# First layer of a four-layer image network: taps in pairs, transposes on VectorE, TensorE in a written order

## The chip, the cores and the metric

The kernel runs on one core of a Trainium2 chip. The metric is the device time of one execution in microseconds; the time of a version is the median of its runs.

## What is computed

Two images of 512 channels and 64 x 64 pixels pass through four attention and pooling layers in float32, each added to its input after a group normalisation. Only the first layer is touched. Its reference, cut to what matters:

```python
q_norm = l2norm(q)                                   # per pixel and head: 8 heads of 64 channels
q_scaled = (q_norm + query_embedding) * softplus(temperature)
k_local = l2norm(k)                                  # then padded, and taken at 3 x 3 neighbours
attn_local = einsum('bhnd,bhndk->bhnk', q_scaled, k_local_patches)     # 9 taps
attn_pool = einsum('bhnd,bhpd->bhnp', q_scaled, l2norm(k_pool))        # 256 pooled keys
attn = softmax(concat([attn_local, attn_pool]))
a_local, a_pool = attn[..., :9], attn[..., 9:]
lt = einsum('bhnd,hdk->bhnk', q_norm, learnable_tokens) + learnable_bias + a_local
x_local = einsum('bhnk,bhndk->bhnd', lt, v_local_patches)
x_pool = einsum('bhnp,bhpd->bhnd', a_pool, v_pool)
out = (x_local + x_pool) @ W_proj + b_proj
```

## The kernel before

An image lies in the on-chip memory as four chunks of 128 channels (two heads each) by 4096 pixels. The class `Local` does the first layer. It cuts a chunk into four units of 1024 pixels (16 image rows), so an image has 16 units. A unit is worked in halves of 512 pixels, the width of one accumulator bank.

`run` is a software pipeline. In each turn of its loop the work of several units is laid side by side as Python generators, and `in_turn` takes one step of each, round after round. In turn `i`, `projections` makes the keys of unit `i+4`, the queries of unit `i+3` and the values of unit `i+1`; `norms` and `normed` normalise what the turn before projected; `tap_products` and `tap_sums` make the nine neighbour scores of unit `i+1`; `attend` does the pooled attention and the softmax denominators of unit `i`; `weigh` applies the nine neighbour weights of unit `i-1`. The loop runs from -4 to 16; turns 0 to 15 have an `attend`.

The order in which the generators emit their instructions is a priority. A scheduler then lays out a fixed sequence for each engine: it takes an instruction when it holds it to be ready, earlier emitted ones first. So on TensorE the work of the stages is interleaved as the scheduler saw fit, not as it is written. Every engine runs its own sequence strictly as laid out and waits on semaphores. All transfers in this part are issued by SyncE's queue.

The steps that the change touches:

- Norms (L2275 to L2308). A product with a 0/1 matrix puts the sums of squares of up to four half units into rows 0 and 1 of four strips of 32 partitions of one bank. ScalarE copies the bank (L2279), TensorE transposes it in four 128 x 128 blocks (L2283), VectorE computes the inverse root in integer and float steps on 32 columns (L2290 to L2298) into the array `wide`, TensorE transposes `wide` back (L2304) and ScalarE copies it (L2306). `normed` spreads two rows over the 128 channels by a product (L2318) and multiplies on VectorE (L2326). `learned` (L2339) makes the token scores and the scaled queries.
- Taps (L2366, L2379). VectorE multiplies the unit's queries with the keys shifted by one tap, 1024 columns at a time, into a ring of three buffers `prods`; TensorE sums each over the channels of a head, two taps at a time into four strips of one bank.
- Denominators (L2433, L2437, L2458). The exponentials of two key blocks are added on GpSimd (L2426), for the second half in place in the exponentials' own buffer; TensorE sums them over keys, into rows that alternate between the two heads, so that 64 rows per half hold only two different values each; VectorE inverts all 512 columns, in two halves.
- Weighing (L2491 to L2510). Each tap's weight is spread to the partitions by a transfer (L2477) into a ring of three buffers, copied to an accumulator bank by ScalarE, multiplied on VectorE and added on GpSimd (L2504).

Accumulator memory: five banks `mm` are shared by the projections, scores, `values`, norms, spreads and the weighing's copies; one bank holds the tap sums, two hold the queries for the tap products.

Of the kernel before, what the change touches and what calls it, by code (L numbers as in the profile page):

```python
# [1914 lines left out]
class Local:  # L1915
# [9 lines left out]
    def __init__(self, net, X, Y, sp_scale, d, wp, yp, pp, ppt, pps):  # L1925
# [20 lines left out]
        self.prods = [whole.take([P, self.UT])] + [new([P, self.UT], f"prod{i}") for i in range(2)]  # L1946
# [19 lines left out]
        self.qn = new([P, self.UT], "qn")  # L1966
# [3 lines left out]
        self.wide = new([P, NT, P], "wide")  # L1970
# [12 lines left out]
        nc.gpsimd.memset(self.wide, 0.0)  # L1983
# [11 lines left out]
    def run(self):  # L1995
# [10 lines left out]
        for i in range(-4, units + 1):  # L2006
# [22 lines left out]
            in_turn(*stages)  # L2029
# [139 lines left out]
    def fetch_output(self):  # L2169

        for _ in range(3):

            yield
        for kc in range(KC):
            self.nc.sync.dma_start(self.sq[kc], self.d["W_proj"][kc * P:(kc + 1) * P, :])
        self.pb = self.kp[:, :2, :].rearrange("p c n -> p (c n)")
        self.nc.sync.dma_start(self.pb, self.d["pb_rows"])
        yield

    def output(self, c4):  # L2180
# [4 lines left out]
        toks = ([self.prods[0], self.prods[1], self.prods[2], self.qs[(units - 2) % 3]] if c4 % 2  # L2185
# [46 lines left out]
    def projections(self, uk, uq, uvs, streams):  # L2232
# [33 lines left out]
    def norms(self, streams, ended):  # L2266
# [27 lines left out]
        for i in range(3):  # L2294
            nc.vector.tensor_tensor(a, n, y, ALU.mult)
            nc.vector.tensor_tensor(a, a, y, ALU.mult)
            dst = self.wide.rearrange("p t (s r) -> p t s r", s=4)[:, :, :, :2] if i == 2 else y
            nc.vector.scalar_tensor_tensor(dst, a, 1.5, y, ALU.add, ALU.mult)  # L2298
        yield
        yield  # L2300
        yield
        ps = self.bank()
        for t in range(NT):
            nc.tensor.transpose(ps[:, t * P:(t + 1) * P], self.wide[:, t, :], self.net.ident)  # L2304
        rows = wp.tile([P, TB], F32, name="n_rows")
        nc.scalar.copy(rows, ps)  # L2306
# [3 lines left out]
    def normed(self, ended):  # L2310

        nc = self.nc
        for _ in range(5):
            yield
        for which in "kq":
# [11 lines left out]
            yield  # L2327
        if mine:
# [27 lines left out]
    def tap_products(self, u):  # L2356
# [5 lines left out]
        qs = qs.rearrange("p (y x) -> p y x", x=W)  # L2362
        y = u % self.UN * self.UY
        for k in range(9):
            dy, dx = divmod(k, 3)
            self.nc.vector.tensor_tensor(  # L2366
                self.prods[k % 3].rearrange("p (y x) -> p y x", x=W), qs,
                self.kx[:, y + dy:y + dy + self.UY, dx:dx + W], ALU.mult)
            yield

    def tap_sums(self, u):
# [3 lines left out]

        def sums(k):
            for j in range(2):
                q = 2 * j + k % 2
                nc.tensor.matmul(ps[32 * q:32 * q + 32, :],  # L2379
                                 self.cst[:, C_TAPW + 16 - 2 * k:C_TAPW + 48 - 2 * k],  # L2380
                                 self.prods[k % 3][:, j * TB:(j + 1) * TB], start=(k < 2),
                                 stop=(k > 6))

        yield
        yield
        for k in range(0, 8, 2):
            sums(k)
            sums(k + 1)
            yield
            if k < 6:  # L2390
                yield
        sums(8)
# [5 lines left out]
    def attend(self, u):  # L2398
# [45 lines left out]
        yield  # L2444
        values(0)
        yield
# [254 lines left out]
```

## Time and profile before

| | |
|---|---|
| median of 5 runs | 5157.76 us (5148.33 to 5165.67) |
| the profiled execution | 5172.35 us, its span 5170.4 us |
| TensorE / VectorE / ScalarE / GpSimd busy | 95 / 59 / 36 / 36% of the span |
| mean granted TensorE clock | 0.978 of full speed |
| first layer's loop, denominators of unit 0 to those of unit 13 | 575.54 us (first image) |

The profile is of one execution. The duration of a TensorE product in it is modelled, and products overlap: the price of a group is the distance from its first start to the start of the next group. A product in float32 appears as two instructions. The tile names `late`, `big` and `mm` are the shared work area, the two image arrays (whose free one lends space to this layer) and the five banks. "Idle before" is the time that an engine waited, with the instruction that released it.

### The profile page before, as it was taken

What the parts mean: (1) busy time and instruction counts of PE and PEld (TensorE: products, weight loads), DVE (VectorE), ACT (ScalarE), POOL (GpSimd) and SP (SyncE); (2) the same over time, 40 slices, a digit from 0 to 9 for tenths busy, and PEclk for the clock granted to TensorE, in tenths of its full rate; (3) what the DMA queues carried; (4) which work ended last, traced back from release to release, by engine and by line L of the source; (5) the groups of instructions that cost most, each with busy time, mean ns of one, the idle gap of its engine ahead of it and who ended that gap; (6) DMA issues with size and microseconds to landing.
All of it is one profiled execution on the core that took longest, in us unless ns stands there. A gap on an engine that the chain in (4) does not pass through costs nothing. (4 is left out here: it accounts for less than half of the span.)

```text
span 5170.4 us, 48736 instructions
## 1 busy us (share of the span) xinstructions
PE 4907.3 (95%) x17299; PEld 2039.7 (39%) x17299; DVE 3068.0 (59%) x3986; ACT 1864.7 (36%) x3547; POOL 1846.5 (36%) x1216
## 2 busy tenths in 40 slices
PE   7999999899998999999999999998999999999998
PEld 3423332555333444433344333335543344444333
DVE  4266777644579633478732677776445795334766
ACT  1245665324422233322112556652343232333221
POOL 0035566500430045454500455565003200454544
PEclk9999999899999999999999999999999999999999
DMA  3035556600000000211120355565000000000111
GB/s 149 2 81 133 145 141 170 171 27 10 1 1 17 1 1 1 66 49 46 60 73 2 93 138 144 144 169 163 19 10 1 1 17 1 1 1 21 39 45 44
DMA packets 124752, 309.88 MB, mean 60 GB/s; under 512 B 20882, under 2 KB 33682, under 8 KB 122964
## 3 DMA queue, kind: packets, MB, share of 16 engines
q1 hardware_dynamic: 124500, 306.68, 21.0%
q8 instruction: 139, 2.28, 0.2%
q14 instruction: 113, 0.93, 0.1%
HBM read 258.11 MB, written 48.50 MB: 59 GB/s over the span
## 5 line engine op out<-in xcount | busy, mean ns | idle before, releaser
L134 PE MATMUL mm<-big,w 128*128 128x512 f32 x2496 | 1164.0, 611 | 9.1 <-DVE late L2458 9.1
L134 PEld LDWEIGHTS mm<-big,w 128*128 128x128 f32 x2496 | 456.4, 192 | 678.2 <-issue 561.5
L2504 POOL TENSOR_TENSOR late<-late,big 128x1024 f32<-128x1024 f32 x192 | 454.4, 2367 | 192.2 <-DVE big L2499 175.3
L1616 POOL TENSOR_TENSOR big<-big 128x512 f32<-128x512 f32 x224 | 278.0, 1274 | 219.2 <-ACT big L1607 219.2
L2426 POOL TENSOR_TENSOR late<-late 128x512 f32<-128x512 f32 x128 | 160.7, 1278 | 516.0 <-ACT late L2415 494.4
L2499 DVE TENSOR_TENSOR big<-big,mm 128x512 f32<-128x512 f32 x384 | 255.8, 682 | 126.9 <-ACT mm L2491 112.9
L2491 ACT COPY mm<-big 128x512 f32<-128x512 f32 x428 | 244.5, 593 | 179.6 <-DMA big<-rows 144.9
L1607 ACT ACTIVATE big<-mm,ed 128x256 f32<-128x256 f32 x512 | 194.0, 490 | 232.7 <-DVE top L1603 200.3
L2504 POOL TENSOR_TENSOR late<-late,tap 128x1024 f32<-128x1024 f32 x96 | 227.3, 2368 | 103.9 <-DVE tap L2499 99.0
L1420 POOL TENSOR_TENSOR wq<-prob 128x512 f32<-128x512 f32 x48 | 70.9, 1501 | 511.3 <-ACT prob L1417 511.3
L1871 PE MATMUL mm<-k,w 128*128 128x512 f32 x512 | 236.8, 606 | 12.4 <-DVE k L1864 7.4
L1603 DVE TENSOR_REDUCE top<-mm 128x1 f32<-128x512 f32 x256 | 159.1, 684 | 148.3 <-PE mm L1535 148.3
L134 PE MATMUL mm<-big,wq 128*128 128x512 f32 x512 | 236.8, 612 | 2.7 <-ACT off_t L1219 2.7
L2366 DVE TENSOR_TENSOR prod<-qs,big 128x1024 f32<-128x1024 f32 x192 | 230.7, 1217 | 8.8 <-PE tap L2379 6.8
L1191 PE MATMUL mm<-big,wo 128*128 128x512 f32 x512 | 234.7, 604 | 0.0
L1581 PE MATMUL mm<-w,big 128*128 128x512 f32 x512 | 234.5, 601 | 0.0
L1346 PE MATMUL acc<-big,diag 128*128 128x512 f32 x512 | 226.6, 601 | 4.6 <-ACT diag L1344 4.6
L1861 DVE RECIPROCAL psD<-psD 128x512 f32<-128x512 f32 x64 | 215.1, 3362 | 1.9
L969 POOL TENSOR_TENSOR group_stats<-group_stats,cst 128x1 f32<-128x1 f32 (+1 forms) x20 | 12.2, 624 | 570.9 <-DVE group_stats L968 539.4
L2379 PE MATMUL tap<-prod,cst 128*32 128x512 f32 x768 | 199.1, 605 | 8.9 <-DVE prod L2366 8.0
L134 PE MATMUL mm<-big,big 128*128 128x512 f32 x464 | 201.7, 594 | 0.5 <-DVE b_sr L1007 0.5
L1417 ACT ACTIVATE prob<-mm 128x512 f32<-128x512 f32 x256 | 133.0, 602 | 171.6 <-PE mm L1414 171.3
(410 smaller groups left out, 8488.5 us busy)
## 6 DMA issues: line engine op xcount, KB each, us to landing
big<-rows SPq DMA_DIRECT2D x428, 256.0 KB, 4.3
tap<-rows SPq DMA_DIRECT2D x212, 256.0 KB, 4.2
yd<-late SPq DMA_DIRECT2D x32, 512.0 KB, 2.9
lost_all<-lost SPq DMA_DIRECT2D x128, 128.0 KB, 3.1
out<-big SPq DMA_DIRECT2D x64, 256.0 KB, 2.0
big<-in_W_kv SPq DMA_DIRECT2D x8, 1024.0 KB, 8.8
rows<-late SPq DMA_DIRECT2D x64, 128.0 KB, 2.3
big<-yd SPq DMA_DIRECT2D x16, 512.0 KB, 5.1
```

What stands on the lines that cost most here:

```text
L134: self.nc.tensor.matmul(ps, w[:, kc, :], X[:, kc, blk * TB:(blk + 1) * TB], start=(kc == 0), stop=(kc == KC - 1))
L1191: nc.tensor.matmul(ps, w[:, kc, oc * P:(oc + 1) * P], att[:, kc, :], start=(kc == 0), stop=(kc == KC - 1))
L1346: nc.tensor.matmul(accs[b], dg, src[:, b * TB:(b + 1) * TB], start=(j == 0), stop=(j == 6))
L1581: nc.tensor.matmul(ps, X[:, kc, lo:lo + P], wv[:, kc, :], start=(kc == 0), stop=(kc == KC - 1))
L1616: nc.gpsimd.tensor_tensor(a, a, part, ALU.add)
L1861: nc.vector.reciprocal(psD, psD)
L1871: nc.tensor.matmul(ps, self.wo[:, kc, oc * P:(oc + 1) * P], qs[:, kc, :], start=(kc == 0), stop=(kc == KC - 1))
L2366: self.nc.vector.tensor_tensor(self.prods[k % 3].rearrange("p (y x) -> p y x", x=W), qs, self.kx[:, y + dy:y + dy + self.UY, dx:dx + W], A ...
L2379: nc.tensor.matmul(ps[32 * q:32 * q + 32, :], self.cst[:, C_TAPW + 16 - 2 * k:C_TAPW + 48 - 2 * k], self.prods[k % 3][:, j * TB:(j + 1) * ...
L2491: nc.scalar.copy(ps, part)
L2499: nc.vector.tensor_tensor(part.rearrange("p (y x) -> p y x", x=W), self.vx[:, y:y + self.UY // 2, dx:dx + W], ps.rearrange("p (y x) -> p y ...
L2504: nc.gpsimd.tensor_tensor(out, out, t, ALU.add)
```

## The change

Four things are changed in `Local`.

The tap products are made two taps at a time: one VectorE instruction over 2 x 1024 columns, with the queries repeated and the keys read at two shifts (`shifted`), into a ring of two buffers of two taps (`pair`). The ninth tap stays alone.

The norms lose both sets of TensorE transposes, both ScalarE copies and the array `wide`. VectorE transposes the bank in place in 32 x 32 blocks, computes the roots in the first columns of each block, and transposes the bank into the buffer `sq[3]`.

The denominators are transposed in place on VectorE in 32 x 32 blocks, so that in each block of 32 columns two hold all the different values; these 32 columns in all are inverted, and a second transpose that reads each pair 16 times writes the full array `recip`.

In turns 0 to 13 TensorE's instructions are laid out in the order in which they are written, and the steps at which the stages emit them change. The fetch of the projection weights in turn 13 starts four steps later, and `qn` and the taps' buffers change places in memory.

```diff
-        self.prods = [whole.take([P, self.UT])] + [new([P, self.UT], f"prod{i}") for i in range(2)]
+        self.prods = [new([P, 2, self.UT], f"prods{i}") for i in range(2)]
...
-        self.qn = new([P, self.UT], "qn")
+        self.qn = whole.take([P, self.UT])
...
-            in_turn(*stages)
+            if 0 <= i < units - 2:
+                with self.net.tc.manual_schedule(engines={mybir.EngineType.PE}):
+                    in_turn(*stages)
+            else:
+                in_turn(*stages)
...
-        for _ in range(3):
+        for _ in range(7):
...
         for step in range(10):
-            if step >= 6:
-                project((uk, uq)[step // 2 - 3], "kq"[step // 2 - 3], step % 2)
-            if step % 3 == 0 and values:
+            if step in (4, 6, 7, 8):
+                i = (4, 6, 7, 8).index(step)
+                project((uk, uq)[i // 2], "kq"[i // 2], i % 2)
+            if step in (0, 2, 5, 9) and values:
...
-        rows = wp.tile([P, TB], F32, name="n_rows")
-        nc.scalar.copy(rows, ps)
-        yield
-        ps = self.bank()
-        for t in range(NT):
-            nc.tensor.transpose(ps[:, t * P:(t + 1) * P], rows[:, t * P:(t + 1) * P],
-                                self.net.ident)
-        sums = ps.rearrange("p (t s r) -> p t s r", t=NT, s=4)
-        n, a = (sums[:, :, :, 2 * i:2 * i + 2] for i in range(2))
-        y = wp.tile([P, NT, 4, 2], F32, name="roots")
+        yield
+        nc.vector.transpose(ps, ps)
+        n, a = (ps.rearrange("p (b r) -> p b r", r=32)[:, :, 2 * i:2 * i + 2] for i in range(2))
+        y = wp.tile([P, TB // 32, 2], F32, name="roots")
...
-            dst = self.wide.rearrange("p t (s r) -> p t s r", s=4)[:, :, :, :2] if i == 2 else y
-            nc.vector.scalar_tensor_tensor(dst, a, 1.5, y, ALU.add, ALU.mult)
-        yield
-        yield
-        yield
-        ps = self.bank()
-        for t in range(NT):
-            nc.tensor.transpose(ps[:, t * P:(t + 1) * P], self.wide[:, t, :], self.net.ident)
-        rows = wp.tile([P, TB], F32, name="n_rows")
-        nc.scalar.copy(rows, ps)
+            nc.vector.scalar_tensor_tensor(n if i == 2 else y, a, 1.5, y, ALU.add, ALU.mult)
+        rows = self.sq[3]
+        nc.vector.transpose(rows, ps)
...
-        for _ in range(5):
+        for _ in range(3):
             yield
...
             yield
+        yield
         if mine:
             self.learned(mine[-1][0][3])
...
-        for k in range(9):
-            dy, dx = divmod(k, 3)
+        for k in range(0, 9, 2):
+            n = min(2, 9 - k)
             self.nc.vector.tensor_tensor(
-                self.prods[k % 3].rearrange("p (y x) -> p y x", x=W), qs,
-                self.kx[:, y + dy:y + dy + self.UY, dx:dx + W], ALU.mult)
-            yield
+                self.pair(u, k)[:, :n].rearrange("p k (y x) -> p k y x", x=W),
+                bcast(qs.rearrange("p (y x) -> p y x", x=W), 1, n),
+                self.shifted(u % self.UN * self.UY, k, n), ALU.mult)
+            yield
+            if n == 2:
+                yield
+
+    def pair(self, u, k):
+        return self.prods[(5 * u + k // 2) % 2]
+
+    def shifted(self, y, k, n):
+        a = self.kx[:, y:y + self.UY, :W]
+        at = lambda k: k // 3 * (W + 2) + k % 3
+        part, rows, cols = a.ap
+        return bass.AP(a.tensor, a.offset + at(k), [part, [at(k + 1) - at(k), n], rows, cols])
...
+        yield
+        for k in range(0, 9, 2):
+            for i in range(min(2, 9 - k)):
+                for j in range(2):
+                    q = 2 * j + i
+                    nc.tensor.matmul(ps[32 * q:32 * q + 32, :],
+                                     self.cst[:, C_TAPW + 16 - 2 * (k + i):][:, :32],
+                                     self.pair(u, k)[:, i, j * TB:(j + 1) * TB],
+                                     start=(k == 0), stop=(k + i > 6))
+            for _ in range((2, 2, 3, 1, 0)[k // 2]):
                 yield
...
         exponentials(0, 1)
         yield
+        yield
         values(0)
-        yield
         exponentials(1, 0)
         yield
         exponentials(1, 1)
         yield
         values(1)
         yield
-        yield
         psD = sums()
-        for i in range(2):
-            part = slice(i * TB // 2, (i + 1) * TB // 2)
-            nc.vector.reciprocal(self.recip[:, part], psD[:, part])
+        nc.vector.transpose(psD, psD)
+        two = psD.rearrange("p (b n r) -> p b n r", n=16, r=2)[:, :, 0]
+        nc.vector.reciprocal(two, two)
+        nc.vector.transpose(self.recip.rearrange("p (b n r) -> p b n r", n=16, r=2),
+                            bcast(two, 2, 16))
         yield
         el = self.el.pop(u)
         nc.vector.tensor_tensor(el, el, self.recip, ALU.mult)
         nc.vector.tensor_tensor(el, el, self.lt.pop(u), ALU.add)
+        yield
         self.spread = self.rows()
```

More of the change, by code (lines that the diff above doesn't have):

```diff
@@ L1969, in __init__ @@
         self.half = new([P, 32], "mhalf32")
-        self.wide = new([P, NT, P], "wide")
         self.qb = new([P, KC], "qe_scaled")
@@ L1982, in __init__ @@
         nc.vector.memset(self.half, -0.5)
-        nc.gpsimd.memset(self.wide, 0.0)
         nc.vector.tensor_tensor(self.qb, self.vec[:, V_QE:V_QE + KC], sp_scale, ALU.mult)
@@ L2184, in output @@
         units = KC * self.UN
-        toks = ([self.prods[0], self.prods[1], self.prods[2], self.qs[(units - 2) % 3]] if c4 % 2
+        toks = ([a[:, i] for a in self.prods for i in range(2)] if c4 % 2
                 else [self.kraw, self.qn,
```

14 lines of the change are left out of this document (removed).

## The prediction

> **What bounds the kernel now.** I read the page's first block, then the busy time in chosen stretches, then TensorE's timeline inside one stretch, and last GpSimd's timeline there.
>
> ```profile
> span 5170.4 us, 48736 instructions
> ...
> PE 4907.3 (95%) x17299; PEld 2039.7 (39%) x17299; DVE 3068.0 (59%) x3986; ACT 1864.7 (36%) x3547; POOL 1846.5 (36%) x1216
> ```
>
> 95% is an average. The change touches only the first layer's loop over 16 units, twice (two images). The denominators' first product (L2433) starts at 306.50 us in the first unit and at 882.04 in the fourteenth; for the second image at 2880.44 and 3452.09. So 13 turns of the loop take 575.54 and 571.65 us: 44.27 and 43.97, mean 44.12 us a turn.
>
> ```profile
> 306.50:882.04 575.54, 563.72 (x2043) 184.51 (x2041) 412.45 (x642) 340.56 (x598) 330.13 (x165) 0.99 0.55 143
> ```
>
> The columns are length, then busy time of TensorE, its weight loads, VectorE, ScalarE, GpSimd. TensorE is busy 98%, VectorE 72%, GpSimd 57%. What ends a turn is TensorE's list of work, so the timeline must say whether that list can shrink and whether it is packed.
>
> ```profile
> 655.31 0.63 PE L2379 MATMUL tap<-prod,cst 128*32 128x512 f32 x3
> 655.75 0.59 PE L2379 MATMUL tap<-big,cst 128*32 128x512 f32 x1
> 655.76 0.61 PE L2379 MATMUL tap<-prod,cst 128*32 128x512 f32 x3
> 656.30 0.66 PE L2304 MATMUL mm<-cst,wide 128*128 128x128 f32 x4
> 656.88 1.94 PE L2421 MATMUL mm<-late,vp 128*64 128x512 f32 x8
> 658.90 1.13 PE L2318 MATMUL mm<-n_rows,cst 2*128 2x512 f32 x4
> 659.96 3.70 PE L134 MATMUL mm<-big,w 128*128 128x512 f32 x8
> 663.59 1.13 PE L2318 MATMUL mm<-n_rows,cst 2*128 2x512 f32 x4
> 664.65 1.94 PE L2433 MATMUL mm<-late,cst 128*64 128x512 f32 x8
> ...
> 671.15 1.07 PE L2339 MATMUL mm<-qn,big 128*32 128x512 f32 x8
> 672.05 1.02 PE L2379 MATMUL tap<-prod,cst 128*32 128x512 f32 x2
> ```
>
> Read the starts, not the durations: a group's price is the next start minus its own. Four transposes cost 0.58 us, `values` 1.9, a projection 3.64, two norm spreads 1.06, a denominators' first part 1.87 (the second, L2437, 1.00), the tokens' product (L2339) 0.90. Two taps together cost 0.99 and a lone tap 0.95: four strips of 32 columns run side by side and a lone tap fills two of them. Elsewhere in this turn scores of one half and key block (L2411) cost 1.06, sums of squares (L2276) 1.00.
>
> **The change part by part.** I count one turn of TensorE in the new order: six projections 21.84, four score groups 4.24, four tap pairs and one lone tap 4.91, `values` twice 3.74, norm spreads twice 2.12, denominators 2.87, tokens 0.90, sums of squares 1.00. Sum 41.62 us. Against 44.12 that is 2.50 us a turn, in three pieces.
>
> *Transposes go.* L2283 and L2304, two groups of four at 0.58: 1.16 us a turn, all on the path. Two ScalarE copies of 0.59 go too; ScalarE is 59% busy, worth nothing by itself.
>
> *Taps stay paired.* The present order issues about three pairs and three lone taps a turn, 5.82 us against 4.91: 0.91 us, if the written order holds.
>
> *The rest, 0.43 us*, is today's idle and slow-clock time, which goes only if the new order has none.
>
> *VectorE's list.* Removed: two reciprocals at 1.726 (3.45 us). Added: a transpose, a 32-column reciprocal, a transpose, and two transposes for the norms. No row has a bare transpose; the nearest is the transposing sum.
>
> ```profile
> L1799 DVE TRANSPOSE_TENSOR_REDUCE sq_cols<-sq 128x16 f32<-128x512 f32 x64 | 43.9, 694 | 26.6 <-POOL sq L1504 25.9 <-PE mm L1810 0.7
> L2458 DVE RECIPROCAL late<-mm 128x256 f32<-128x256 f32 x64 | 107.8, 1726 | 11.5 <-PE mm L2437 11.0
> ```
>
> [...] The reciprocal of 512 columns (L1861) is 3.362, of 256 is 1.726: 6.39 ns a column and 0.09 fixed, so 0.30 for 32. New: 4 x 0.69 + 0.30 = 3.06, against 3.45. Taps: nine at 1.217 become four of about 2.28 (1.066 us per 1024 elements, 0.15 fixed) and one of 1.217, so 10.34 for 10.95. [...] The denominators' own chain, sums to `el`, shortens from 3.45 to 1.7 us.
>
> On the pairing: VectorE is 72% busy here, and in the layout below no pair falls due sooner than some 10 us after its buffer is free. [...] I go by the row and charge nothing.
>
> *Steps moved.* The denominators and `el` come one step earlier, while the spread's two transfers and the first two fetches stay in steps eight and nine: SyncE's queue keeps its order against the weighing's fetches, but `el` waits up to a step in it; rows land about as early in the turn as now, so nothing. Norm spreads and tokens come one to two steps earlier, so their four multiplications (0.68) and the 1.24 us rescaling on ScalarE move forward into time when those engines are no busier. Projections are parted by spreads and denominators, so their ScalarE copies (0.69 and 0.68) bunch less. I charge these nothing; without that cover one step of each would cost a bank wait, which (c) below bounds.
>
> *The fixed order.* 14 turns of each image. Laid out by the prices above, from the first scores at 0: scores, value 4.7; squares 5.7, scores 6.8, taps 7.8; value 11.4; `values` 13.3, scores 14.3, taps 15.3, key spread 16.4; scores 17.4, projection 21.1, query spread 22.1; `values` 24.0, taps 25.0; denominators 27.9, projection 31.5, tokens 32.4; projection 36.0; taps, projection 40.7; last tap 41.6. What TensorE may now wait for, and everything behind it on TensorE waits too:
>
> (a) Denominators after `values`. They need GpSimd's sum of the two key blocks in place, so it starts only after `values` at 24.0. Only a tap pair, 1.0 us, lies between. Today `values` end at about 658.8 and the denominators start at 664.65, and in between GpSimd does this:
>
> ```profile
> 658.29 2.37 POOL L2504 TENSOR_TENSOR late<-late,tap 128x1024 f32<-128x1024 f32 x1 [2.72 <-DVE tap L2499]
> 660.62 2.51 POOL L2426 TENSOR_TENSOR late<-late 128x512 f32<-128x512 f32 x2
> ```
>
> GpSimd idle: the second head's sum lands 2.5 us after `values`, wait about 0.4. A tap addition of 2.37 just begun: 2.8. I take 0.8 (57% busy, half an addition left).
>
> (b) Key spread. Today the norms run from the transposes' end at 602.5 to the last root at 610.94: 8.4 us, mostly other VectorE work let in between. With a transpose on each side 9.8 us, against 9.6 between squares' end and key spread. Bounds 0 and 2; I take 0.3.
>
> (c) Five banks for scores, spreads and weighing copies around 13 to 18 us. Bounds 0 and 1.5; I take 0.3.
>
> Period 41.62 + 1.4 = 43.0 us, 1.1 less than now: 28 turns, 31 us.
>
> *Outside the fixed turns.* Three more turns an image lose 1.16 of transposes and about 1 us of waits around the two copies (0.76, 0.82, 0.99 and 0.73 us of idle are seen at 232 to 268): six turns, 12 us less 3 for transposes in sequence. The last turns lose idle behind the long reciprocal (2.68 us at 886, 2.92 at 3456), partly paid back: 3 us. The projection weights fetched four steps later have some 15 us before use: nothing. Together 12.
>
> **Sum.** The profiled execution took 5172.35 us, span 5170.4, the five runs' median 5157.76: the profile is 0.3% long. 31 + 12 = 43 us: 5129 in a profile, 5115 in the median.
>
> **The rivals.**
>
> *No waits at all.* If GpSimd is always free at 24 us and VectorE's norms keep time, the turn is 41.62: 2.50 x 28 + 15 = 85 us, 5073. For: today's waits on TensorE in ten turns sum to a few us. Against: (a) is too tight for zero.
>
> *Weighing becomes the bound.* Fetches for a unit begin at 636.17 and its output transfer issues at 679.45: 43.3 us, three buffers, each reused only after its GpSimd addition; the next unit's fetch went out after that. The long reciprocal held one step back some 2 us, which goes. If the chain keeps 43.3, later turns follow it or the lag lands in the last turns: 0.8 x 28 less some lag, about 10 to 20 us gained, 5143.
>
> *Slower.* The place is (a). TensorE did stop once for long in the early turns:
>
> ```profile
> 384.62 0.63 PE L2304 MATMUL mm<-cst,wide 128*128 128x128 f32 x4 [2.09 <-DVE wide L2298]
> 385.18 2.92 PE L2421 MATMUL mm<-late,vp 128*64 128x512 f32 x8
> 388.03 2.08 PE L2318 MATMUL mm<-n_rows,cst 2*128 2x512 f32 x4
> 390.04 6.77 PE L134 MATMUL mm<-big,w 128*128 128x512 f32 x8
> ```
>
> After 2.09 us of idle three groups took 11.55 us (385.18 to 396.73) instead of 6.6: the clock had halved, 5 us more. If GpSimd always begins a tap addition first, (a) costs 2.8 every turn; with 0.6 elsewhere 45.0, and one slow spell in three turns makes 46.7: 2.6 x 28 - 12 = 60 us slower, 5218. It decides from 2.5 us of waits a turn; without slow spells it is 5170. [...]
>
> **How the numbers follow.** Forecast with its bounds, 5095 to 5135: 0.38. No waits: 0.20. Weighing: 0.18, of which 0.07 ends within 0.2%. Slower: 0.24 with milder forms. A measurement of this kernel tells about 0.2%, 10 us. Faster 0.69, same 0.07, slower 0.24. The range must reach past "no waits" and into the slower case: 5068 to 5190 leaves out about 0.05 below and 0.14 above.
>
> **What would show it.** L2283 and L2304 gone; starts of the denominators about 43 us apart over the fixed turns; transposes near 0.69 us and reciprocals of 0.3 us; tap products in eight instructions at a time except the last; idle on TensorE, if any, ahead of L2433's successor, released by GpSimd. Wrong in kind if the period is above 44.1, if halved-clock stretches repeat there, or if the gain of the fixed turns comes back as a longer tail after the fourteenth unit.

## The result and the profile after

The changed kernel takes 5168.43 us in the median of 31 runs against 5157.22 of 53: the ratio is 1.0022 [1.0016, 1.0029], some 11 us slower. The profiled execution took 5172.82 us (that of before, 5172.35, lay 15 us above its own median). The first lines of its page, to set against those of before:

```profile
span 5171.0 us, 48104 instructions
...
PE 4867.7 (94%) x17027; PEld 2001.0 (39%) x17027; DVE 3070.0 (59%) x3958; ACT 1819.2 (35%) x3479; POOL 1849.0 (36%) x1214
```

TensorE lost 272 instructions and 39.6 us of work, and the span is as long as before: idle time took the place of the work. The busy time over the same stretch as before, from the denominators of the first unit to those of the fourteenth (length, then TensorE, weight loads, VectorE, ScalarE, GpSimd; the first number behind them is the granted clock):

```profile
302.50:885.40 582.90, 548.78 (x1928) 169.91 (x1924) 413.98 (x629) 322.29 (x571) 333.64 (x167) 0.97 0.53 141
```

TensorE is busy 14.9 us less than before and idle 34.1 us instead of 11.8, so the stretch is 7.4 us longer (13.3 for the second image, 584.9 us). The mean clock in it fell from 0.99 to 0.97. Outside this stretch the change gained: the two turns behind it are together 4.4 us shorter in the first image and 1.2 in the second, and the opening turns, up to the first denominators, are 4.0 us shorter in the first image and 6.6 in the second. What is left over, mostly code that the change does not touch, is 3.9 us shorter in this pair of profiles, so that the two spans come out alike although the medians differ by 11 us.

In between the loop falls into a strict period: the starts of the denominators at 617.32, 661.75 and 706.18 us are 44.43 us apart, where the prediction said 43.0. TensorE's timeline in one such turn shows two stops. An entry in brackets is the idle time ahead of the group and what ended it.

```profile
649.53 1.06 PE L2380 MATMUL tap<-prods,cst 128*32 128x512 f32 x8
650.52 1.13 PE L2306 MATMUL mm<-sq,cst 2*128 2x512 f32 x4
651.58 1.13 PE L2404 MATMUL mm<-big,kp 64*128 64x512 f32 x4
654.20 3.70 PE L134 MATMUL mm<-big,w 128*128 128x512 f32 x8 [1.49 <-DVE big L2314]
657.83 1.13 PE L2306 MATMUL mm<-sq,cst 2*128 2x512 f32 x4
658.89 1.94 PE L2414 MATMUL mm<-late,vp 128*64 128x512 f32 x8
660.76 1.07 PE L2380 MATMUL tap<-prods,cst 128*32 128x512 f32 x8
661.75 2.87 PE L2426 MATMUL mm<-late,cst 128*64 128x512 f32 x8
```

The first stop is open: 1.49 us ahead of a projection, which waits for the key multiplications (L2314) to give a bank back. The second hides in the length of a group: the denominators' first part takes 2.87 us, where it took 1.94 before. VectorE and GpSimd at these two places:

```profile
650.66 2.29 DVE L2353 TENSOR_TENSOR prods<-qs,big 128x2048 f32<-128x2048 f32 x1 [0.23 <-PE tap L2380]
652.87 0.68 DVE L2494 TENSOR_TENSOR big<-big,mm 128x512 f32<-128x512 f32 x1
653.46 1.28 DVE L2314 TENSOR_TENSOR big<-big,mm 128x512 f32<-128x512 f32 x2
```

```profile
656.13 2.35 POOL L2499 TENSOR_TENSOR late<-late,tap 128x1024 f32<-128x1024 f32 x1
660.97 2.52 POOL L2419 TENSOR_TENSOR late<-late 128x512 f32<-128x512 f32 x2 [2.49 <-PE mm L2414]
```

The spread of the key norms ends at about 651.6, but VectorE has just begun a pair of tap products, takes a weighing product behind it, and comes to the key multiplications at 653.46. The projection starts at 654.20, right behind the first of the two (654.15). GpSimd stands idle for 2.49 us until `values` release the exponentials, and its two sums then end at 663.5, after the denominators could have begun.

In the turns behind the first and the second denominators of each image there is a third stop: TensorE waits for the norms' last transpose, and the products behind it run slow (here at a granted clock of 0.50 up to 341.58 us, and 1.00 behind it).

```profile
335.46 2.08 PE L2306 MATMUL mm<-sq,cst 2*128 2x512 f32 x4 [4.61 <-DVE sq L2294]
337.47 2.08 PE L2404 MATMUL mm<-big,kp 64*128 64x512 f32 x4
339.48 4.73 PE L134 MATMUL mm<-big,w 128*128 128x512 f32 x8
```

The account of a turn, as the prediction made it (next start minus own, us; mean of 16 turns, in each image the eight from the denominators of unit 3 to those of unit 11):

| | turn | projections | scores | taps | values | denominators | spreads | rest |
|---|---|---|---|---|---|---|---|---|
| before | 44.12 | 21.59 | 4.57 | 5.77 | 4.08 | 2.87 | 2.11 | 3.12 |
| the prediction's list | 41.62 | 21.84 | 4.24 | 4.91 | 3.74 | 2.87 | 2.12 | 1.90 |
| after | 44.54 | 21.89 | 5.80 | 5.21 | 3.74 | 3.80 | 2.12 | 2.00 |

The rest is tokens, squares and, before, transposes. So transposes (1.22), taps (0.56) and `values` (0.34) were saved, and scores (1.23), denominators (0.93) and projections (0.30) gave 2.46 us back.

### The profile page after: what moved, and what is told of

Same layout as the page of the kernel before. It is cut to its first block, busy times and chain, and to the rows that moved or that the text cites. A ratio compares the mean times of both kernels' runs of the same rounds, so it can differ in the third digit from the quotient of the medians.

```text
span 5171.0 us, 48104 instructions
## 1 busy us (share of the span) xinstructions
PE 4867.7 (94%) x17027; PEld 2001.0 (39%) x17027; DVE 3070.0 (59%) x3958; ACT 1819.2 (35%) x3479; POOL 1849.0 (36%) x1214
## 5 line engine op out<-in xcount | busy, mean ns | idle before, releaser
L2353 DVE TENSOR_TENSOR prods<-qs,big 128x2048 f32<-128x2048 f32 (+1 forms) x160 | 331.6, 2075 | 111.0 <-PE tap L2380 100.5
L2380 PE MATMUL tap<-prods,cst 128*32 128x512 f32 x1152 | 181.2, 623 | 19.8 <-DVE prods L2353 19.8
```

Source lines behind the costliest of these rows:

```text
L2353: self.nc.vector.tensor_tensor(self.pair(u, k)[:, :n].rearrange("p k (y x) -> p k y x", x=W), bcast(qs.rearrange("p (y x) -> p y x", x=W), ...
```

## The experiments

All ratios are to the kernel before, measured on the same chip in the same round of runs, with the 95% interval; the turn is the mean of the same 16 turns, in us. Each expectation explains its own letters; a letter does not mean the same in the first eight runs and in the later ones.

### Is it the written order?

**e1_free**: the changed kernel, TensorE's order left to the scheduler.

```diff
-            if 0 <= i < units - 2:
-                with self.net.tc.manual_schedule(engines={mybir.EngineType.PE}):
-                    in_turn(*stages)
-            else:
-                in_turn(*stages)
+            in_turn(*stages)
```

> The changed kernel without the written order of TensorE; all else of the change stays. Theory A (the written order costs what the rest of the change brings: in a settled turn of 44.44 us TensorE stands 1.56 us for a bank that VectorE frees late, 0.93 us for GpSimd's sum and about 0.3 elsewhere): the scheduler parts these neighbours again, a turn falls to about 43.0 us, the 28 turns save some 40 us, and the kernel is 0.5 to 1% faster than before, 5110 to 5135 us. Theory B (the costs lie in the rest: pair products and transposes lengthen VectorE's list and hold banks, whoever orders TensorE): time stays within 0.3% of the changed kernel, 5155 to 5185 us, and idle on TensorE released by VectorE stays. Theory C (the weighing's chain of transfers sets the turn): a turn stays at 44 us with idle spread elsewhere.

**e9_fixed**: the same lines the other way round, in the kernel before: its steps in their written order in turns 0 to 13, and nothing else.

> The kernel before with only TensorE's written order in turns 0 to 13, all steps, tap products, transposes and reciprocals as before. TensorE's list is then 42.78 us a turn with four tap pairs and one lone tap, and a spread, a tap pair, a projection and the query spread lie between the last values and the denominators, so GpSimd's sum has over 6 us. Theory D: waits stay small, a turn is 42.9 to 43.6 us, kernel 15 to 35 us faster than before, 5123 to 5143 us. Rival (a written order as such costs, whatever its steps): turns above 44.5 us, slower than before.

e1_free: 5171.98 us, 1.0024 [1.0012, 1.0036], turn 44.81. The scheduler too put the denominators close behind `values` (4.88 us for them). e9_fixed: 5174.67 us, 1.0039 [1.0026, 1.0052], turn 44.81: taps fall from 5.77 to 4.98, and scores rise to 5.41 and projections to 21.96. The order costs nothing that its absence would give back, and alone it makes the kernel slower. Of the expectations, theory B of e1_free had the time right, and the rival of e9_fixed came true.

### Each of the other parts alone

**e4_norms**: the kernel before with the norms' transposes on VectorE. **e5_den**: the kernel before with the new denominators. Both take that part of the change's diff and nothing else, except that in e4_norms the roots go to a buffer of their own.

> The kernel before with one part of the change: norms by VectorE's transposes instead of TensorE's and ScalarE's copies (no pairs, no written order, old reciprocals). Theory A: 1.16 us less TensorE work a turn, all of it on the path: 25 to 45 us faster than before, 5112 to 5133 us. Theory B: the transposes and the chain they lengthen on VectorE give most of it back: within 10 us of before.

> The kernel before with only the denominators of the change (transpose, 32 columns inverted, transpose) instead of the two reciprocals. VectorE saves 1.6 us a turn (0.73 + 0.37 + 0.72 against 3.45). Theory D: the waits of TensorE on the long reciprocal go (2 to 3 us in each image's last turns), settled turns hardly change because TensorE is full there: 5 to 20 us faster than before, 5137 to 5153 us. Rival (the scheduler lays out everything anew and pairs taps by chance): a change of either sign up to 30 us, with the count of lone taps in a turn changed.

e4_norms: 5165.09 us, 1.0017 [1.0002, 1.0032], turn 44.80. The transposes' 1.22 us are gone, but the scheduler pairs fewer taps (7.09 us instead of 5.77) and `values` rise to 4.38. e5_den: 5164.51 us, 1.0013 [1.0001, 1.0024], turn 44.67, taps 6.63. Each part alone loses about what the whole loses: in e4_norms in the size that theory B gave but by lone taps, in e5_den as its rival said.

### Pairs, and the steps

**e2_single**: the changed kernel with the products one tap at a time, in the same buffers.

```diff
-            self.nc.vector.tensor_tensor(
-                self.pair(u, k)[:, :n]..., bcast(qs..., 1, n), self.shifted(..., k, n), ALU.mult)
+            for i in range(n):
+                self.nc.vector.tensor_tensor(
+                    self.pair(u, k)[:, i:i + 1]..., bcast(qs..., 1, 1), self.shifted(..., k + i, 1), ALU.mult)
```

> The changed kernel with each tap product made alone (nine instructions of 1024 columns into the same two-tap buffers); written order kept. Theory A says the 1.56 us wait is a 2.29 us pair product that VectorE takes just before the key spread's multiplications: with 1.2 us products the wait falls to 0.3 to 0.9 us, the two early waits of 4.5 us on the norms shrink, a turn takes 43.4 to 43.9 us, kernel 5125 to 5150 us. A rival (five banks are simply too few there) keeps the wait near 1.5 us and the time within 0.2% of the changed kernel.

5142.87 us, 0.9962 [0.9946, 0.9977]: faster than before, and 26 us below the changed kernel by medians (31 by the ratios). The stop behind the scores falls from 1.49 to 0.99 us, because one product of 1.22 us and not a pair of 2.29 stands ahead of the key multiplications:

```profile
649.48 1.13 PE L2405 MATMUL mm<-big,kp 64*128 64x512 f32 x4
651.60 3.70 PE L134 MATMUL mm<-big,w 128*128 128x512 f32 x8 [0.99 <-DVE big L2314]
```

The settled turn is 43.93 instead of 44.43, and the first image's last two turns take 97.1 instead of 100.1 us. The key multiplications come 1.1 us earlier against the spread, but only 0.50 of it shows: the projection now starts behind the second of them (it ends at 651.55), where in the changed kernel it started behind the first. The two long stops on the norms did not shrink, as this expectation held; they are 4.8 us here.

**e3b_proj** moves one projection from step 6 to step 5, **e3_moved** also the yields of `tap_sums`, **e7_single_moved** is e2_single with both:

```diff
-            if step in (4, 6, 7, 8):
-                i = (4, 6, 7, 8).index(step)
+            if step in (4, 5, 7, 8):
+                i = (4, 5, 7, 8).index(step)
...
-            for _ in range((2, 2, 3, 1, 0)[k // 2]):
+            for _ in range((3, 1, 3, 1, 0)[k // 2]):
```

> The changed kernel with only the second key projection moved ahead of the denominators (pairs kept, tap sums where the change has them). Theory D: the 0.93 us inside the denominators goes, the 1.5 us wait behind the key spread stays: a settled turn 43.4 to 43.7 us, kernel 20 to 30 us below the changed one, 5138 to 5150 us. Theory C: a turn stays within 0.2 us of 44.4 and the wait turns up elsewhere.

> The changed kernel with two steps of the written order moved: the second tap pair's sum one step later (behind the key spread instead of ahead of it, so that the pair product it releases comes after the key multiplications), and the second key projection ahead of the denominators (3.64 us between the last values and the denominators). Theory A: both waits go, a turn is 41.9 to 42.4 us, 28 turns save 55 to 70 us, kernel 5095 to 5120 us, about 1% faster than before. Theory C (weighing's chain of about 43.3 us sets the turn): a turn stays above 43.2 us although neither wait is left at its place.

> The changed kernel with tap products made one at a time and both steps of the written order moved (second tap sum one step later, second key projection ahead of the denominators). Theory D (TensorE's waits come from what stands ahead on VectorE and GpSimd: a 2.29 us pair product before the key spread and inside the norms' chain, a GpSimd sum 1 us before it is needed): the gains of the two earlier runs add up, a settled turn is 42.2 to 42.8 us against 44.44, kernel 5085 to 5120 us. Theory C (weighing sets the turn at about 43.3 us): a turn stays at 43.2 us or more, kernel 5125 to 5145 us, no better than the single taps alone by more than 0.3%.

| | median | ratio | turn | projections | scores | taps | denominators | spreads |
|---|---|---|---|---|---|---|---|---|
| e3b_proj | 5168.24 | 1.0016 [1.0001, 1.0032] | 44.69 | 22.40 | 6.18 | 5.40 | 2.87 | 2.11 |
| e3_moved | 5162.76 | 1.0005 [0.9991, 1.0019] | 44.23 | 22.15 | 4.78 | 5.87 | 2.87 | 2.84 |
| e7_single_moved | 5150.03 | 0.9983 [0.9970, 0.9996] | 44.14 | 21.85 | 5.14 | 5.85 | 2.87 | 2.72 |

In all three the denominators no longer wait (2.87 us), and all three are slower than theories A and D said. Part of the time is back in another column. The rest lies where the mean of 16 turns does not reach. In the profiles, the 13 turns of both images together are 28.5 (e3_moved) and 13.8 us (e3b_proj) shorter than the changed kernel's and 19.6 us (e7_single_moved) shorter than e2_single's, but the openings, from the norm of the pooled tokens to the first denominators, where the scheduler still orders most of TensorE's work, are 18.4, 11.4 and 16.6 us longer.

### More banks, and what came of it

**x1_seven**, **x8_single7** (on e2_single) and **x6_befseven** (on the kernel before) give `mm` seven banks by leaving out the copy of the queries; **x3_nocopy** leaves out ScalarE's copies of the weights.

```diff
-                tc.tile_pool(name="l0m", bufs=5, space=PSUM) as pp, \
+                tc.tile_pool(name="l0m", bufs=7, space=PSUM) as pp, \
...
-        qs = self.pps.tile([P, self.UT], F32, name="qs")
-        (two ScalarE copies into qs)
+        qs = self.qs[u % 3]
```

```diff
-            banks = [self.bank() for _ in range(2)]
-            for ps, part in zip(banks, parts):
-                nc.scalar.copy(ps, part)
+            banks = parts
```

> The changed kernel with seven banks mm instead of five: the two banks that held a copy of the queries for the tap products go to mm, and the tap products read the queries from SBUF; ScalarE's two copies a unit are gone with them. In the changed kernel a turn is 44.54 us where TensorE's own list is 41.6, and 1.49 us of the difference is a stop between the score groups that a bank ends. Theory B (the five banks are what turns the late VectorE steps into waits of TensorE): that stop and those behind it go, the turn falls to 43.0 us, 28 x 1.5 = 42 us less, median near 5125 (5115 to 5140). Rival C (the weighing's own chain of transfer, copy, product and sum sets the turn): the waits move elsewhere and the turn stays within 0.3 us of 44.5, median 5160 to 5175. Rival E (VectorE's order: the pair product itself is late or dearer): as C, and if the pair product from two SBUF operands takes more than the 2.29 us it takes now, slower than the changed kernel.

> The changed kernel with five banks, but the weighing multiplies straight from the fetched rows in SBUF: ScalarE's copies to banks are left out, 18 bank uses fewer a turn and one step less in the weighing's chain. Theory B (banks): as with seven banks, because the weighing no longer holds any of the five: the stop of 1.49 us goes, turn near 43.0, median 5115 to 5140. Theory C (the weighing's chain sets the turn): the same fall or a larger one, and then seven banks alone must not give it. Rival E (VectorE's order): the product from two SBUF operands takes more than the 0.68 us it takes from a bank, VectorE gets later and the turn stays at 44 or above, median 5160 to 5185.

> The changed kernel with tap products one at a time (which alone gave 5142.9) and seven banks mm. Theory B: both causes of late evacuation are taken, the settled turn falls from 43.9 to 42.4 us (list 41.6 and 0.8 for the denominators), median 5142.9 - 28 x 1.4 = near 5103 (5095 to 5120). Rival C: the turn stays at 43.5 or above and the median within 10 us of 5143.

> The kernel before with seven banks mm and the tap products reading the queries from SBUF, all else as it was. Theory B, if the banks bind the kernel before too: its turn of 44.12 us loses most of what its exponentials and taps lie above the list (0.3 to 0.9 us), median 5130 to 5148. Rival (in the kernel before the scheduler's own order already keeps TensorE fed, so banks cost it nothing): within 8 us of 5157.

In the order of the expectations: 5242.08 us, 1.0164 [1.0147, 1.0181], turn 47.31; 5410.35, 1.0485 [1.0468, 1.0502]; 5216.79, 1.0107 [1.0091, 1.0124], turn 45.53; 5232.35, 1.0136 [1.0120, 1.0153], turn 47.26. All four are slower, so none of the theories was tested cleanly: the edit made the instructions themselves longer. The groups of x8_single7 between 400 and 900 us (busy time, mean ns of one, idle before):

```profile
L2350 DVE TENSOR_TENSOR prods<-big 128x1024 f32<-128x1024 f32 x99 | 210.5, 2127 | 18.6 <-PE tap L2377 17.6
```

```profile
L2416 POOL TENSOR_TENSOR late<-late 128x512 f32<-128x512 f32 x44 | 76.8, 1766 | 62.3 <-ACT late L2405 55.5 <-PE mm L2411 6.8
```

In e2_single the same tap product takes 1219 ns and GpSimd's sum 1278. Two of the runs still say something, against each other. With seven banks the scores of x8_single7 take 4.38 us against e2_single's 5.30, near the bare 4.24. But x1_seven, which has seven banks too and a pair product of 3.11 us, keeps the stop: 1.7 to 2.2 us ahead of the same projection, ended by VectorE, and scores of 6.30. And x8_single7 stops in each turn for 0.74 to 0.76 us one group earlier instead, ahead of the key spread, until ScalarE's weighing copy is done.

### Two attempts to part banks from VectorE

**y3_nobanks**: the weighing multiplies by the queries' banks, without copies and without banks of its own; it leaves out the weights, so its output is not that of the layer. **y4_half**: VectorE weighs half of each tap and leaves out the other half.

```diff
-        qs = self.pps.tile([P, self.UT], F32, name="qs")
+        qs = self.held = self.pps.tile([P, self.UT], F32, name="qs")
...
-            banks = [self.bank() for _ in range(2)]
-            for ps, part in zip(banks, parts):
-                nc.scalar.copy(ps, part)
+            banks = [self.held[:, j * TB:(j + 1) * TB] for j in range(2)]
```

```diff
-                    self.vx[:, y:y + self.UY // 2, dx:dx + W],
+                    self.vx[:, y:y + 4, dx:dx + W],
```

> The changed kernel, but the weighing multiplies by the copy of the queries that lies in its own two banks in place of the weights, so that it neither takes any of the five banks mm nor uses ScalarE (20 copies of 0.6 us a turn fewer), while VectorE's products keep their 0.68 us and the transfers and GpSimd's sums stay: the output of the first layer is another one, and the time is to be read as that of a weighing without banks. Theory B (the five banks, a third of whose uses are the weighing's, turn VectorE's lateness into stops of TensorE): the exponentials fall from 5.80 to 4.3 us, the turn from 44.54 to 42.8 (41.6 and 0.9 for the denominators and 0.3), median near 5120 (5105 to 5135). Rival E (VectorE's order alone: the banks of the scores are held by VectorE's own late steps, not by the weighing's): the turn stays within 0.4 us of 44.5, median 5155 to 5175. It can also come out slower: the next unit's copy of the queries must then wait for the last weighing product.

> The changed kernel, but VectorE weighs only 4 of the 8 image rows of each half (128 x 256 instead of 128 x 512); the rest of the weighed tap stays unweighed, so the first layer's output is another one. VectorE's load falls by some 18 x 0.33 = 6 us a turn (an estimate from half of 0.68 us), the banks' uses, ScalarE's copies, the transfers and GpSimd's sums stay. Theory B: a bank of the weighing is held only 0.3 us less, the stop stays at 1 us or more, turn 43.8 to 44.5, median 5145 to 5170. Rival E (VectorE's order and load): the key multiplications come earlier, the exponentials fall to 4.3 to 4.8 us and the turn to 43.2, median 5120 to 5140.

5300.90 us, 1.0268 [1.0244, 1.0292], turn 52.25; 5231.80 us, 1.0143 [1.0123, 1.0163], turn 47.79. Both are slower than the ranges of either theory, and neither tells the theories apart. In y4_half VectorE had less to do (0.41 us instead of 0.68 a product) and GpSimd's sums came later: the denominators took 6.99 us of a turn. In y3_nobanks the key spread waited 5.9 to 7.1 us a turn for the norms, in single turns up to 9.8. Whether banks or VectorE's order alone make the stop stays open on this evidence.

### Taking a wait away

**y1_single_own** (on e2_single) and **y2_own** (on the changed kernel) let GpSimd write the first head's second sum into `recip`, which is free then, so that only one sum waits for `values`.

```diff
-            dst = prob[1, 1] if j else self.halves
+            dst = self.late(prob) if j else self.halves
...
+    def late(self, prob):
+        return self.recip, prob[1, 1][1]
```

> The changed kernel with tap products one at a time, and GpSimd's sum of the second half's first head written into the array recip (free at that time) instead of in place over the exponentials that the values still read, so that only the second head's sum (1.28 us) waits for the values. Theory 1 (each wait of TensorE costs by itself): the denominators' wait of 0.93 us a turn goes, the turn falls from 44.22 to 43.3 us, 28 x 0.93 = 26 us less than 5142.9, near 5117 (5110 to 5128). Rival 2 (a wait that is taken away comes back as a later wait for a bank, as in the run with moved projection steps): the denominators are back at 2.87 us but the exponentials or projections rise by as much, turn 44.0 to 44.4, median 5135 to 5150.

> The changed kernel with the same edit of GpSimd's sum alone (tap products in pairs). Theory 1: turn from 44.54 to 43.6 us, median near 5142 (5135 to 5153). Rival 2: turn 44.2 to 44.7, median 5160 to 5175.

y1_single_own: 5125.94 us, 0.9937 [0.9918, 0.9956], the fastest version here, faster than both kernels. y2_own: 5156.25 us, 0.9994 [0.9983, 1.0005]. The denominators are 2.87 us in both. Of the 0.93 us a turn that this frees, the turn keeps 0.40 in y1_single_own (43.85 against e2_single's 44.25; the 44.22 of its expectation took the turns one unit later in the second image) and 0.02 in y2_own (44.52 against 44.54). Where the rest goes can be read in TensorE's timeline of y1_single_own. Two projections after the same stop, one turn apart:

```profile
643.90 3.70 PE L134 MATMUL mm<-big,w 128*128 128x512 f32 x8 [0.99 <-DVE big L2314]
```

```profile
686.90 5.40 PE L134 MATMUL mm<-big,w 128*128 128x512 f32 x8 [0.99 <-DVE big L2314]
```

and the same two stretches in the view by windows, where the number after the engines' busy times is the granted clock:

```profile
643.90:647.60 3.70, 3.70 (x10) 1.51 (x10) 2.27 (x3) 0.87 (x2) 3.70 (x3) 1.00 0.29 87
686.90:692.30 5.40, 5.40 (x10) 2.10 (x10) 2.27 (x3) 0.95 (x2) 4.78 (x3) 0.68 0.39 100
```

Same products, same stop, but a clock of 0.68: 1.70 us lost. In y1_single_own 8 of 18 such stops are followed by a slow projection and its turns are 43.0 or 44.7 us; in y2_own it is 9 of 18 and the turns 43.5 or 45.2; in e2_single it is 3 and in the changed kernel 1 of 18. So the wait did go, 0.93 us in each turn without a slow projection; what came back is the slow clock.

### Moving the key multiplications ahead

**z1_normed** (on y1_single_own) and **z3_after_normed** (on the changed kernel) place `normed` ahead of `tap_sums` in the list of stages, so that the key spread and, on VectorE, the key multiplications come ahead of the next tap product.

```diff
+            stages.append(self.normed(ended))
             if ahead is not None:
                 stages.append(self.tap_sums(ahead))
...
-            stages.append(self.normed(ended))
```

> Products one at a time, GpSimd's sum in recip, and the generator normed placed ahead of tap_sums in the round, so that TensorE spreads the key norms 1.06 us earlier (before the tap sums instead of behind them) and VectorE takes the two key multiplications ahead of the next tap product. In the run without this edit, settled turns are 43.0 us, and 44.7 us where the stop of 0.99 us behind the last score group is followed by eight products at 5.40 instead of 3.70 us. Theory D (the stop is what stands ahead of the key multiplications on VectorE): the stop falls under 0.3 us, the slow products behind it go, every settled turn is 42.0 to 42.4 us, median near 5085 (5075 to 5105). Rival 2 (the stop comes back elsewhere, now at the next bank or at a tap sum): turns 43.0 or more, median 5115 to 5135.

> The changed kernel with this one edit, normed ahead of tap_sums; products in pairs and the denominators as they are. The settled turn is 44.44 us now, 1.49 us of it the stop behind the last score group. Theory D: that stop goes to 0.3 us or less, turn 43.0 to 43.3 us, 28 x 1.2 to 1.4 = 34 to 40 us less than 5168.4, median near 5132 (5122 to 5145): the 43.0 us of the prediction. Rival 2: the pair product now stands ahead of the query multiplications (1.28 us later) and the stop moves there, turn 44.0 to 44.6, median 5155 to 5172.

z1_normed: 5150.43 us, 0.9988 [0.9975, 1.0002], turn 44.03. z3_after_normed: 5184.66 us, 1.0048 [1.0030, 1.0067], turn 45.80. The stop behind the last score group is gone in both (scores 4.45 and 4.53 us a turn), and both are slower than without the edit. In z1_normed's timeline:

```profile
603.20 1.93 PE L2306 MATMUL mm<-sq,cst 2*128 2x512 f32 x4
605.06 1.74 PE L2381 MATMUL tap<-prods,cst 128*32 128x512 f32 x8
606.73 2.08 PE L2405 MATMUL mm<-big,kp 64*128 64x512 f32 x4
608.74 1.87 PE L2306 MATMUL mm<-sq,cst 2*128 2x512 f32 x4
```

```profile
603.20:605.00 1.80, 1.80 (x6) 0.58 (x4) 0.72 (x2) 1.74 (x4) 0.56 (x1) 1.00 0.88 230
605.00:608.70 3.70, 3.70 (x13) 0.66 (x12) 3.70 (x5) 0.59 (x1) 2.37 (x1) 0.54 0.58 143
608.70:610.50 1.80, 1.80 (x6) 0.58 (x4) 1.12 (x3) 1.58 (x3) 0.99 (x1) 0.99 0.56 180
```

The two spreads, 1.13 us each in the changed kernel, take 1.9 with the clock at 1.00 and 0.99: each of these pairs of products holds a wait. In the trace the second product starts 0.81 and 0.75 us behind the first, released by ScalarE's exponentials (L2409), which read a score bank, in the one place where the scores, two spreads and the weighing's copies all ask for the five banks (spreads 3.69 us a turn instead of 2.12). Between them the clock is 0.54. In kind the rival of these two expectations holds, though both runs are slower than it said: the stop was not taken away but moved, from one stop of 0.99 us into two short ones and a slow spell.

## Why the prediction was wrong

**The list was right.** It had the transposes gone and the taps paired, 41.62 us. Its items were met to 0.1 us (21.89, 3.74, 2.12, 1.00; the denominators 2.87 where they do not wait), but for the taps, 5.21 against 4.91. VectorE's prices held too: transposes 0.716 to 0.732 us for 0.69, the figure of the transposing sum, the 32-column reciprocal 0.366 for 0.30, pairs 2.289 for 2.28.

**(a), the denominators, was right in its place and its cause**: 0.93 us for 0.8, by GpSimd's sum. That the size fits is partly luck. The 0.8 held half a tap addition, which does not stand in the way, since GpSimd is waiting there; for an idle GpSimd the prediction had about 0.4, and 0.93 is what that case costs. The slower rival had this place at 2.8 us.

**(c), the five banks, is the term that failed**: 0.3 us taken, 1.49 measured in every settled turn, which was the upper bound. With the numbers of the table: 43.02 predicted; scores 1.26 above what (c) allowed; taps 0.30, denominators 0.13, tokens 0.10, projections 0.05 more; 0.30 less for (b), which is nothing in settled turns. That makes 44.56, and 44.54 was measured. The working looked at what TensorE wants in that stretch and not at what VectorE has ahead of the instructions that return the banks. By the prediction's own sign, a period above 44.1 us, it was wrong in kind.

**Charging nothing for the pairs** is the same error from its other side. The buffer is free early enough, as the prediction says; but the pair that VectorE begins at 650.66 takes 2.29 us, and the key multiplications come behind it, at 653.46. e2_single shows the price: 26 us by medians. The sign of the result hangs on it, since with single products the rest of the change is faster than before (0.9962). The engine was 71% busy in the loop and still held TensorE up for 1.49 us in each settled turn, and shorter instructions were better although they cost 0.15 us more a pair. Of the 26 us, 0.50 us of each settled turn and 3 us in the last two turns of each image are seen; the rest is not accounted for.

**(b), the norms**, is nothing in the settled turns and 4.5 to 4.6 us twice in each image, in the turns behind the first and second denominators, with slow products behind it. Tap products and weighing products let in between its steps stretch VectorE's chain to 11.6 us (323.70 to 335.31), where the prediction had 9.8. It is not the pairs alone, since e2_single stops as long there. The bound of 2 was too low, but it falls on few turns.

**Steps moved, charged nothing**, belongs to (c): between the key spread and a projection that asks for a bank now lies one score group of 1.06 us. Moving steps by hand (five runs) gained in the loop in three of them, but the gain was lost again, most of it in the opening turns; the other two lost in the loop itself.

**Outside the fixed turns** 12 us were expected; the openings gave 4.0 and 6.6 and the last turns 4.4 and 1.2 in this pair of profiles, 16 in all. Of the forecast of 43 us this part came about, and a little more.

**The rivals.** "No waits" fell with (c). "Weighing becomes the bound" fell: in the changed kernel the first fetch of a unit waits for the rows to land (29.4 us over ten turns) and not for a buffer, and y1_single_own, with the same weighing, has turns of 43.0. "Slower" was right in its sign and wrong in its place; that its time without slow spells, 5170, is so near the 5168 measured is luck. Its other half, that slow clock follows short stops, was seen (0.68 over 5.40 us behind a stop of 0.99 us in y1_single_own), though seldom in the changed kernel itself (1 of 18).

**What stays open** is which of the two, too few banks or VectorE's order, is behind the 44 us that the versions without longer instructions come to. For banks speak x8_single7's scores and z1_normed's spreads, for VectorE's order e2_single and the stop that x1_seven keeps. No run changed the one without the other. Nor was it tried to lay out VectorE's order by hand.

## What to carry to other kernels

Where TensorE hands banks to another engine, price a longer instruction on that engine by what is queued behind it, not by its own busy time or by when its buffer is free: here a product of 2.29 instead of 1.22 us ahead of the instructions that return a bank cost 26 us in all, on an engine that was idle 29% of the time. Work taken from the bounding engine shows in the time only if the engines that feed it can follow in that stretch: 2.1 us a turn were taken from TensorE's work, and 2.5 came back, most of it as waits. To remove one wait, break its dependency (a sum in an array of its own gained 17 and 12 us by medians); reordering moved the waits or lengthened the opening turns in all five runs that tried it, and at best gained 6 us by medians (e3_moved). And look at the whole loop: a mean over settled turns did not show what the openings lost.

## What the runs showed of the hardware

**Products with both operands in SBUF.** With one operand in an accumulator bank the tap product takes 1.22 us (e2_single), with both in SBUF 2.13 (x8_single7), and GpSimd's additions in the same stretch take 1.77 instead of 1.28. The weighing product went from 0.68 to 1.25 us (x3_nocopy). The copies into banks, which look like waste, pay for themselves here: without the weighing's copies the changed kernel's ratio is 1.0485 instead of 1.0022. Why both engines' instructions take longer, no run here shows.

**Slow clock after short stops.** A stop of 0.99 us was followed by 5.40 us at a clock of 0.68 (y1_single_own, 686.90 us), and the same stop one turn earlier by 3.70 us at 1.00. In the changed kernel a stop of 1.49 us was followed by 5.40 us at 0.68 (3307.20 us), and the same stop one turn earlier by 3.70 us at 1.00. z1_normed ran 3.70 us at 0.54 with no idle time ahead of it in the records. With the 0.50 that the changed kernel's clock shows from 334.77 to 341.58 us, the parts at the low clock are, by my estimate, 5.40 x 0.32 / 0.5 = 3.5 and 3.70 x 0.46 / 0.5 = 3.4 us, each costing 1.7. So the length of the stop alone did not decide whether slow clock followed: behind stops of 0.99 us it did in 8 of 18 in y1_single_own and 3 of 18 in e2_single, behind stops of 1.49 us in 9 of 18 in y2_own and 1 of 18 in the changed kernel. What decided it was not tested.
